# An output projection in three rounded passes one block earlier, with the weight splits that it needs moved into the first block

## The chip, the core and the metric

The kernel runs on one core of a Trainium2 chip. The metric is the device time of one execution in microseconds (us). Engine names are those of the profile: PE is TensorE (matmuls), PEld its weight loads, DVE is VectorE, ACT is ScalarE, POOL is GpSimd, and SP is SyncE, which here only issues DMAs.

## The reference, cut to what matters

The input `x` is (4, 1024, 512) in fp32. A layernorm `xn` of it goes through a time-mix part with a scan over time, and through a feed-forward part with a GELU, and both are added to `x`.

```python
def _L0_attn_ref(x, time_mix_k, time_mix_r, Wk, Wr, Wv, time_decay, ...):
    xx = concatenate([x[:, 1:2, :], x[:, :-1, :]], axis=1) - x
    k = einsum('btc,hc->bth', x + xx * time_mix_k, Wk)     # HIDDEN = 704
    r = einsum('btc,hc->bth', x + xx * time_mix_r, Wr)
    w = exp(-exp(time_decay))
    # scan over time: state = state * w + relu(k_t); out_t = state * r_t
    out = einsum('bth,ch->btc', out, Wv)
    ...  # layernorm of out with ln_gamma, ln_beta

def _L0_ffn_ref(x, W0, bias0, W1, bias1):                  # N = 2048
    X = x.reshape(-1, H).astype(float16)
    D = dot(X.astype(float32), W0.T) + bias0
    D = gelu(D, approximate=False).astype(float16)
    E = dot(D.astype(float32), W1.T) + bias1
    return E.astype(float16)

xn = layernorm(x)
return x + _L0_attn_ref(xn, ...) + _L0_ffn_ref(xn, ...)
```

All weights are fp32. The hidden width 704 is five tiles of 128 and a half tile of 64.

## The kernel before

**Blocks and chunks.** The 4096 tokens are worked off in eight blocks of 512 (`blocks`, numbered 0 to 7; `LAST` is 7). Inside a block the loop `for n in range(NN)` runs over the 16 chunks of 128 of the feed-forward width. In each chunk PE is given, in this order: `up` for the chunk two ahead (`AHEAD = 2`; 8 matmuls at L817), `down` for chunk n (8 matmuls at L839), and one "piece" of the time-mix part of the same block: a k or r projection, a half tile, or one quarter of the output projection (`out_piece`, at n = 12, 13, 14, 15). The chunk in which this stands is called its stage.

**Exact products from rounded operands.** The fast matmuls here take fp32r operands. A weight is therefore split once into terms: W0 and W1 into a high and a low one (`split`, L190 on ACT, L191 on DVE), Wk, Wr and Wv into three (`split_kr`, `split_wv`: three operations on DVE, two on ACT). Each fp32r matmul is one instruction of one pass; a plain fp32 matmul is one instruction of several passes.

**What block 0 does beside.** Block 0 uses the raw Wk and Wr, and prepares the terms for the others. It loads raw W1 chunks two to three chunks ahead (`load_w1_raw`, L229), splits each (`load_w1`), and stores the terms to device memory (`w1d`). It splits W0; the high term stays on the chip for good (`w0h`). It splits tiles of Wk and Wr (`split_kr`, L256, L264, L266 to L268) and stores their terms (`krd`). From block 1 on, `load_w1` and `load_kr` read them back.

**W0's low term.** It stays on the chip in blocks 0 and 1. `store_w0l(g)` queues the store of one quarter of it (four DMAs of 256 KB, to `w0d`) in block 1 at n = 0, 4, 8 and 12. From block 2 on, `load_w0l` reads it one chunk (256 KB) at a time.

**Output projection.** `RAW_OUT` is 2: blocks 0 and 1 use the raw Wv in plain fp32 (`out_full`, L713: five matmuls for each of the four quarters s; `out_halves`, L725: 64x64 pieces for the half tile). Blocks 2 to 7 use `out_three_pass`: per quarter ten fp32r matmuls into `oa` (L754), five into `ob` (L762) and two more into `ob` (L764). For that, `gated` also splits each state tile g into three terms (`split_x`), and Wv is split in block 1 at n = 11, 12, 13, 13, 13 and 15.

**Order.** The order on every engine is written by hand inside `tc.manual_schedule`. `put(n, fn, ...)` appends work to chunk n; `woven` interleaves it on DVE and ACT with what must follow the previous piece. Stores are not issued where they arise: `split_kr`, `load_w1` and `store_w0l` append them to the list `stores`, and `store_weights()` at the end of the chunk issues the whole list on SP, in order. In a chunk of block 0 the raw load stands ahead of that on the same queue:

```python
            if i == 0 and ahead + 1 < NN:
                load_w1_raw(ahead + 1)
            woven(works, jobs + bg[n])
            if i == 0:
                waiting.append((d, load_w1(*nxt)))
            store_weights()
```

So the work that is put to chunk n (a `split_kr`, say) stands on DVE and ACT ahead of the split of the W1 chunk n + 2.

**Start and end.** `first_inputs` keeps PE turning with `busy` matmuls on zeros until the first transposes of x come. At the end, `finish(LAST, s, ...)` adds quarters s = 0 and 1 on POOL and stores each as two halves; quarters 2 and 3 are done in column halves (`end_by_columns`), each stored alone. All these stores are issued by SP.

Of the kernel before, what the change touches and what calls it, by code (L numbers as in the profile page):

```python
# [17 lines left out]
P = 128  # L18
# [4 lines left out]
def time_mix_and_gelu_ffn(  # L23
# [26 lines left out]

    nc = tc.nc
    B, T, C = x.shape
    HID = wkT.shape[1]
# [4 lines left out]
    NN = N // P  # L61
    Q = 32
    QS = 62
    RAW_OUT = 2
    S = 4096.0
    MASK = -4096

# [16 lines left out]
    def part(name, dtype=F32R, tag="q", bufs=QS):  # L84
        return wide.tile([P, TB], dtype, tag=tag, name=name, bufs=bufs)
# [124 lines left out]
            stores.append((w0l_dram[g][:, :, c, :].bitcast(F32), terms.bitcast(F32)))  # L210

    def load_w0l(i, n):
        if i > 1:
            w0ls[i, n] = part(f"w0l_{i}_{n}", tag="w0l", bufs=3)
            g, k = divmod(n, G)
            src = w0l_dram[g][:, k].rearrange("p c k -> p (c k)")
            nc.sync.dma_start(w0ls[i, n].bitcast(F32), src.bitcast(F32))
# [38 lines left out]
        nc.vector.tensor_scalar(u.bitcast(I32), raw.bitcast(I32), MASK, None, ALU.bitwise_and)  # L256
        return u

    def split_kr(block, kind, h):
        raw = raw_w.pop((kind, h)).rearrange("p c k -> p (c k)")  # L260
        name = f"{kind}_{h}"
        u = truncated(raw, f"wu_{name}")
        d = temp(f"wd_{name}")
        nc.vector.tensor_sub(d, raw, u)  # L264
        terms = [part(f"wt_{name}_{p}", tag="kr", bufs=6) for p in range(3)]
        nc.scalar.copy(terms[0], u)  # L266
        nc.scalar.activation(terms[1], d, AF.Copy, scale=S)
        nc.vector.scalar_tensor_tensor(terms[2], d, -S, u, ALU.mult, ALU.add)  # L268
        for p in range(3):
            stores.append((kr_dram[kind, h][p].bitcast(F32), terms[p].bitcast(F32)))  # L270
        return [t.rearrange("p (c k) -> p c k", c=NC) for t in terms]
# [138 lines left out]
    def first_inputs(xs, behind):  # L410
# [69 lines left out]
        with tc.manual_schedule(  # L480
            engines={nc.scalar.engine, nc.vector.engine, nc.tensor.engine}
        ):
            nc.scalar.activation(dev[:, 1:2], eps_sb, AF.Sqrt)
            busy(9)
            nc.tensor.transpose(mix_t, mix_rows, ident[: 2 * NC, : 2 * NC])
            first_stats()
            nc.scalar.copy(mix_sb, mix_t)
            nc.scalar.activation(rest_sb, mix_t, AF.Identity, bias=1.0, scale=-1.0)
            turned(0)
            busy(1)  # L490
            pks = [bank(f"pk_0_{h}") for h in range(FIRST)]
            groups = [(0,), (1,), (2, 3), ()]
            for tiles, following in zip(groups, groups[1:]):
                cols = slice(tiles[0] * P, (tiles[-1] + 1) * P)
                for c in range(NC):
                    if c == NC // 2 + (tiles == (0,)):
                        for s in following:
                            normalized(s)
                    mixed_first(0, c, cols.start, cols.stop)
                for c in range(NC):  # L500
                    if c == NC - len(following):
                        for s in following:
                            turned(s)
                    products(c, cols)
                if tiles == (0,):
                    stats(2)
                    stats(3)
                elif tiles == (1,):
                    nc.tensor.transpose(late_t, late_rows, ident[: ND + NN, : ND + NN])
            for c in range(NC):  # L510
                scaled, added = mixed_first(1, c, 0, TB)
            nc.scalar.copy(late_sb, late_t)
            nc.scalar.activation(w_sb, w_sb, AF.Exp)
            scaled = nc.scalar.activation(w_sb, w_sb, AF.Exp, scale=-1.0)
# [281 lines left out]
        nc.vector.tensor_add(e16, sum_, (b1_sb if base is None else base)[:, cols])  # L796
        return e16

    def finish(i, s, e16, cols=slice(0, C), stores=1, adder=nc.vector):
        z = zs[i][:, s, :]  # L800
        b, rows = tokens_of(i, s)
        adder.tensor_tensor(z[:, cols], z[:, cols], e16, ALU.add)
        width = (cols.stop - cols.start) // stores
        for c0 in range(cols.start, cols.stop, width):
            cut = slice(c0, c0 + width)
            nc.sync.dma_start(out[b, rows, cut], z[:, cut])


    def up(i, n):
        pd = bank(f"pd_{i}_{n}")  # L810
        g, k = divmod(n, G)
        cols = slice(k * P, (k + 1) * P)
        low = w0ls.pop((i, n)) if i > 1 else None
        for c in range(NC):
            wl = w0l[c, g][:, cols] if i < 2 else low[:, c * P : (c + 1) * P]
            for p, w in enumerate((w0h[c, g][:, cols], wl)):
                nc.tensor.matmul(  # L817
                    pd,
                    w,
                    xf[c],  # L820
                    start=(c == 0 and p == 0),
                    stop=(c == NC - 1 and p == 1),
                )

        def after():
            d16 = const.tile([P, TB], F16, tag="d16", name=f"d16_{i}_{n}")
            nc.scalar.activation(d16, pd, AF.Gelu, bias=b0_sb[:, n : n + 1])  # L827
            if i == LAST and n >= NN - 2:
                d = part(f"d_{i}_{n}")
            else:  # L830
                d = part(f"d_{i}_{n}", tag="d", bufs=3)
            nc.scalar.copy(d, d16)  # L832
            return d

        return after
# [66 lines left out]
    with tc.manual_schedule(engines=engines):  # L902
        for i in range(len(blocks)):
# [6 lines left out]
                bg[n].append(lambda: fn(*args))  # L910

            def fetch_kr(block, kind, h):
                fetch = split_kr if (kind, h) in raw_w else load_kr
                ks[block, kind, h] = fetch(block, kind, h)

            def fetch_x():
                state["x"] = load_x(j, "x")
# [20 lines left out]
            if i == 0:  # L938
# [11 lines left out]
                    put(5 + c, split_w0, 3, c)  # L950
                put(1, stats, *range(NS))
                put(3, lambda: norm_apply(j, state["x"]))
                for n, *which in ((1, 0, 1), (3, 0, 2), (5, 0, 3), (7, 0, 4), (7, 1, 1)):
                    put(n, split_kr, 1, *which)
                put(4, turn, 0, 1)
                put(5, turn, 1, 5)
# [2 lines left out]
                put(9, turn, 11, 16)  # L959
                put(9, load_late_constants)  # L960
                put(12, split_half)
                mix_at = (11, 12, 13, 15)
            else:
                order = [(0, h) for h in range(NF)] + [(1, h) for h in range(NF)]
                for k, (kind, h) in enumerate(order):
                    if k == NF:
                        for half in range(2):
                            piece(half_at[half], half_pass, i, half)
                    piece(full_at[k], three_pass, i, kind, h)
                    if k > 1:  # L970
                        split_here = (kind, h) in raw_w
                        put(full_at[k - 2 + split_here], fetch_kr, i, kind, h)
                xr_at = {1: (2, 3, 4, 5), LAST: (1, 2, 2, 3)}.get(i, (2, 2, 3, 3))
                for c, n in enumerate(xr_at):
                    put(n, split_xr, i, c)
                if j <= LAST:
                    put(1 if i == 1 else 2, fetch_x)
                    for s in range(NS):
                        put(2 + s // 2 if i == 1 else 4, stats, s)
                    put(4 if i == 1 else 5, lambda: norm_apply(j, state["x"]))  # L980
                    turns = (4, 6, 4, 2) if i == 1 else (4, 5, 4, 3)
                    for k in range(sum(turns)):
                        unit = next(n for n in range(4) if k < sum(turns[: n + 1]))
                        put(6 + unit, turn, k, k + 1)
                mix_at = (10, 12, 13, 15) if i == 1 else (10, 12, 13, 14)
            if i == 1:
                for g in range(NN // G):
                    put(4 * g, store_w0l, g)
                for h, n in enumerate((11, 12, 13, 13, 13, 15)):
                    put(n, split_wv, h)  # L990
            for s, n in enumerate(out_at):
                piece(n, out_piece, i, s)
            put(11 if j <= LAST else 2, fetch_residual)
            if j <= LAST:
                for c in range(NC):
                    put((10, 10, 11, 12)[c], x16, j, c)
                for c, n in enumerate(mix_at):
                    early[n].append((j, c))
                    put(n, mixed, j, c)
                    put(n + (n == 10), split_xk, j, c)  # L1000
                put(13, fetch_kr, j, 0, 0)
                put(14, fetch_kr, j, 0, 1)

# [44 lines left out]
    with tc.manual_schedule(engines={nc.tensor.engine, nc.vector.engine}):  # L1048
# [5 lines left out]
        for s in range(NS):  # L1054
            if s in by_columns:
                end_by_columns(s, chunks, bases[s])
                continue
            if s == 0:
                for some in (chunks[:-1], chunks[-1:]):
                    for whole in range(NS):  # L1060
                        if whole not in by_columns:
                            for n, operands in some:
                                down(n, whole, *operands)
            e16 = rounded(LAST, s, pe[s])
            finish(LAST, s, e16, stores=2, adder=nc.gpsimd)


# [41 lines left out]
```

## Time and profile before

| what | value |
|---|---|
| median of 3 runs | 867.98 us (867.32 to 868.24) |
| the profiled execution's own time | 866.75 us |
| span of its core in the profile | 864.9 us |
| granted clock of PE, mean | 0.999 |
| DVE busy | 669.1 us (77%) |
| ACT busy | 430.3 us (50%) |
| POOL busy | 75.2 us (9%) |
| DMA, mean over the span | 227 GB/s |

The profiled execution lasted 866.75 us, of which the profile's span is 864.9; the rest, 1.85 us, lies around the span. All times inside the execution are counted from the span's start. The "busy" of an engine is the sum over its instructions; an engine can be busy nearly always and yet not set the end, or the other way round, which is why the chain of waits is read with it.

### The profile page before, as it was taken

To read this page: it belongs to the slowest core of one execution; us is meant where nothing else is said; L and a number is where in the kernel's file an instruction comes from. 1 tells how busy PE (TensorE), PEld (TensorE's weight loads), DVE (VectorE), ACT (ScalarE), POOL (GpSimd) and SP (SyncE) were. 2 spreads that over 40 slices of the span, in tenths; PEclk is the share of its full clock that TensorE was granted. 3 is DMA by queue.
4 is the path that set the end of the run, shared out by engine and by line. 5 is a ranking of instruction groups with operands and counts; after the bars stand their busy time and mean duration, and the time that the engine had idled before them with its cause. 6 is when DMAs were issued, how large, how long until landed. Compare 5 with 4: busy or idle time off the path is not lost.

```text
span 864.9 us, 11076 instructions
## 1 busy us (share of the span) xinstructions
PE 859.0 (99%) x3734; PEld 684.6 (79%) x3734; DVE 669.1 (77%) x1092; ACT 430.3 (50%) x729; POOL 75.2 (9%) x145
## 2 busy tenths in 40 slices
PE   9999999999999999999999999999999999999997
PEld 8666658887588888888888888888888888888886
DVE  7678866897877978778887888778886887876546
ACT  6855723556544464444635456254553446544422
POOL 1000000000011002000021001100011200200002
PEclk9999999999999999999999999999999999999999
DMA  9777947866577745967559665696656966578524
GB/s 283 279 266 256 326 135 256 292 193 221 182 250 265 234 165 181 309 227 253 176 167 332 212 212 197 206 327 200 218 198 202 319 211 214 170 250 282 189 103 135
DMA packets 101173, 196.59 MB, mean 227 GB/s; under 512 B 11103, under 2 KB 25724, under 8 KB 101116
## 3 DMA queue, kind: packets, MB, share of 16 engines
q1 hardware_dynamic: 100956, 195.74, 67.5%
q8 instruction: 30, 0.49, 0.2%
q14 instruction: 27, 0.22, 0.1%
q10 hardware_dynamic: 160, 0.14, 0.0%
HBM read 167.00 MB, written 28.84 MB: 226 GB/s over the span
## 4 chain that ended last, share of the span: by engine, by line
PE 98%; DVE 1%; DMA 0%; issue 0%; ACT 0%; ACTq 0%
PE pd L817 27%; PE pe L839 26%; PE pa L657 15%; PE pb L408 7%; PE oa L754 6%; PE po L713 4%; PE ob L762 3%; PE ph L686 3%; PE pr L408 2%; PE pk L408 2%; PE ob L764 1%; PE po L725 0%; PE pkr L631 0%; DMA x<-in_L_attn_x 0%; PE end L839 0%; DVE xk L467 0%
## 5 line engine op out<-in xcount | busy, mean ns | idle before, releaser
L839 PE MATMUL pe<-w,d 128*128 128x512 f32 x1008 | 248.8, 389 | 0.0
L839 PEld LDWEIGHTS pe<-w,d 128*128 128x128 f32 x1008 | 189.1, 188 | 39.4
L817 PE MATMUL pd<-xf,w0h 128*128 128x512 f32 x512 | 203.5, 398 | 0.0
L817 PE MATMUL pd<-xf,w0l 128*128 128x512 f32 x512 | 199.3, 389 | 0.0
L827 ACT ACTIVATE d<-pd,late_sb 128x512 f16<-128x512 f32 x128 | 87.8, 686 | 166.9 <-PE pd L817 166.7
L817 PEld LDWEIGHTS pd<-xf,w0h 128*128 128x128 f32 x512 | 96.1, 188 | 25.8 <-issue 4.9
L817 PEld LDWEIGHTS pd<-xf,w0l 128*128 128x128 f32 x512 | 96.2, 188 | 21.7 <-issue 1.9
L670 DVE SCALAR_TENSOR_TENSOR y<-pb,a 128x512 f32<-128x512 f32 x70 | 48.4, 691 | 65.6 <-PE pb L408 64.7
L669 ACT ACTIVATE a<-pa 128x512 f32<-128x512 f32 x70 | 41.9, 598 | 84.1 <-PE pa L657 83.8
L832 ACT CAST d<-d 128x512 fp32r<-128x512 f16 x128 | 79.6, 622 | 4.1
L352 DVE STREAM_TRANSPOSE xnT<-x 32x512 f32<-32x512 f32 x112 | 78.7, 702 | 2.1
L320 POOL TENSOR_SCALAR ry<-mvy 128x1 f32<-128x1 f32 x32 | 17.2, 537 | 432.1 <-DVE mvy L327 432.1
L657 PE MATMUL pa<-hk,kr 128*128 128x512 f32 x140 | 54.5, 389 | 0.0
L657 PE MATMUL pa<-lk,kr 128*128 128x512 f32 x140 | 54.5, 389 | 0.0
L657 PE MATMUL pa<-hr,kr 128*128 128x512 f32 x128 | 49.8, 389 | 0.0
L657 PE MATMUL pa<-lr,kr 128*128 128x512 f32 x128 | 49.8, 389 | 0.0
L754 PE MATMUL oa<-wv,hg 128*128 128x512 f32 x120 | 46.7, 389 | 0.0
L754 PE MATMUL oa<-wv,lg 128*128 128x512 f32 x120 | 46.7, 389 | 0.0
L672 ACT ACTIVATE y<-y 128x512 f32<-128x512 f32 x35 | 22.1, 633 | 47.3 <-DVE y L670 47.3
L408 PE MATMUL pb<-mk,kr 128*128 128x512 f32 x140 | 37.4, 389 | 0.0
L713 PE MATMUL po<-wvraw,g 128*128 128x512 f32 x80 | 35.6, 592 | 0.0
L769 DVE SCALAR_TENSOR_TENSOR oy<-ob,oa 128x512 f32<-128x512 f32 x24 | 16.6, 692 | 23.2 <-PE ob L764 23.2
(167 smaller groups left out, 1332.5 us busy)
## 6 DMA issues: line engine op xcount, KB each, us to landing
w<-w1d SPq DMA_DIRECT2D x110, 512.0 KB, 3.7
kr<-krd SPq DMA_DIRECT2D x201, 256.0 KB, 4.9
w0l<-w0d SPq DMA_DIRECT2D x96, 256.0 KB, 4.3
w1d<-w SPq DMA_DIRECT2D x16, 512.0 KB, 4.0
xres<-in_L_attn_x SPq DMA_DIRECT2D x32, 256.0 KB, 5.0
x<-in_L_attn_x SPq DMA_DIRECT2D x31, 256.0 KB, 5.4
krd<-wt SPq DMA_DIRECT2D x30, 256.0 KB, 2.8
out<-xres SPq DMA_DIRECT2D x28, 256.0 KB, 5.1
```

What stands on the lines that cost most here:

```text
L352: nc.vector.transpose(dst[i * Q : (i + 1) * Q, :, :, j, :], src[j * Q : (j + 1) * Q, :, :, i, :],)
L408: return nc.tensor.matmul(dst, w[:, c, :], src, start=(c == 0), stop=(c == NC - 1))
L657: nc.tensor.matmul(pa, w[p][:, c, :], xs[j, c][p], start=(c == 0 and p == 0), stop=(c == NC - 1 and p == 1),)
L669: nc.scalar.activation(a, pa, AF.Copy, scale=1.0 + 1.0 / S)
L670: nc.vector.scalar_tensor_tensor(y, pb, -1.0 / S, a, ALU.mult, ALU.add)
L686: nc.tensor.matmul(pa, w[:, c].rearrange("p two k -> p (two k)"), xs[j, c][p], start=(c == 0 and p == 0), stop=(c == NC - 1 and p == 1),)
L713: nc.tensor.matmul(pos[s], gs[i, h][:, s * P : (s + 1) * P], wv_raw[h], start=(h == 0), stop=False,)
L754: nc.tensor.matmul(pa, gs[i, h][p][:, cols], wv[h][p], start=(h == 0 and p == 0), stop=(h == NF - 1 and p == 1),)
L817: nc.tensor.matmul(pd, w, xf[c], start=(c == 0 and p == 0), stop=(c == NC - 1 and p == 1),)
L827: nc.scalar.activation(d16, pd, AF.Gelu, bias=b0_sb[:, n : n + 1])
L832: nc.scalar.copy(d, d16)
L839: nc.tensor.matmul(pe[s] if sum_ is None else sum_, d[:, s * P : (s + 1) * P], w1[p][:, cols], start=(n == first and p == 0), stop=(n == e ...
```

## The change

`RAW_OUT` becomes 1, so block 1 takes `out_three_pass` too, and its state tiles are split. Five of the six Wv splits move to block 0 (n = 12, 13, 15, 15, 15), the sixth to block 1 at n = 4. W0's low term is stored in block 0 at n = 1, 2, 13 and 14 and read per chunk from block 1 on. The splits of Wr's tiles 2 and 3 move from block 1 to n = 1 and n = 5 of block 0; that of Wr's tile 4 stays in block 1 and writes to other buffers. In block 1 the splits of xr and the transposes of the next x stand at other chunks. At the start one `busy` matmul stands ahead of the first four transposes and two behind them, where there was one behind. At the end the stores of quarters 0 and 1 are whole and are issued by ACT.

```diff
-    RAW_OUT = 2
+    RAW_OUT = 1
+    WV_FIRST = {0: 12, 1: 13, 2: 15, 3: 15, 5: 15}
...
     def load_w0l(i, n):
-        if i > 1:
+        if i > 0:
...
-    def split_kr(block, kind, h):
+    def split_kr(block, kind, h, **home):
...
-        terms = [part(f"wt_{name}_{p}", tag="kr", bufs=6) for p in range(3)]
+        home = home or dict(tag="kr", bufs=6)
+        terms = [part(f"wt_{name}_{p}", **home) for p in range(3)]
...
+            busy(1)
             turned(0)
-            busy(1)
+            busy(2)
...
-    def finish(i, s, e16, cols=slice(0, C), stores=1, adder=nc.vector):
+    def finish(i, s, e16, cols=slice(0, C), adder=nc.vector, queue=nc.sync):
...
-        width = (cols.stop - cols.start) // stores
-        for c0 in range(cols.start, cols.stop, width):
-            cut = slice(c0, c0 + width)
-            nc.sync.dma_start(out[b, rows, cut], z[:, cut])
+        queue.dma_start(out[b, rows, cols], z[:, cols])
...
-        low = w0ls.pop((i, n)) if i > 1 else None
+        low = w0ls.pop((i, n)) if i > 0 else None
...
-                for n, *which in ((1, 0, 1), (3, 0, 2), (5, 0, 3), (7, 0, 4), (7, 1, 1)):
+                for n, *which in (
+                    (1, 0, 1), (1, 1, 2), (3, 0, 2), (5, 0, 3), (5, 1, 3), (7, 0, 4), (7, 1, 1)
+                ):
                     put(n, split_kr, 1, *which)
...
+                for g, n in enumerate((1, 2, 13, 14)):
+                    put(n, store_w0l, g)
...
-                    if k > 1:
-                        split_here = (kind, h) in raw_w
-                        put(full_at[k - 2 + split_here], fetch_kr, i, kind, h)
-                xr_at = {1: (2, 3, 4, 5), LAST: (1, 2, 2, 3)}.get(i, (2, 2, 3, 3))
+                    if (kind, h) in raw_w:
+                        put(2, fetch_kr, i, kind, h)
+                    elif k > 1:
+                        put(full_at[k - 2], fetch_kr, i, kind, h)
+                xr_at = {1: (1, 2, 3, 3), LAST: (1, 2, 2, 3)}.get(i, (2, 2, 3, 3))
...
-                    turns = (4, 6, 4, 2) if i == 1 else (4, 5, 4, 3)
+                    turns = (2, 4, 4, 4, 2) if i == 1 else (0, 4, 5, 4, 3)
...
-            if i == 1:
-                for g in range(NN // G):
-                    put(4 * g, store_w0l, g)
-                for h, n in enumerate((11, 12, 13, 13, 13, 15)):
-                    put(n, split_wv, h)
...
+                for h, n in {0: WV_FIRST, 1: {NF - 1: 4}}.get(i, {}).items():
+                    put(n, split_wv, h)
...
-            finish(LAST, s, e16, stores=2, adder=nc.gpsimd)
+            finish(LAST, s, e16, adder=nc.gpsimd, queue=nc.scalar)
```

More of the change, by code (lines that the diff above doesn't have):

```diff
@@ L812, in up @@
         cols = slice(k * P, (k + 1) * P)
-        low = w0ls.pop((i, n)) if i > 1 else None
+        low = w0ls.pop((i, n)) if i > 0 else None
         for c in range(NC):
-            wl = w0l[c, g][:, cols] if i < 2 else low[:, c * P : (c + 1) * P]
+            wl = low[:, c * P : (c + 1) * P] if i > 0 else w0l[c, g][:, cols]
             for p, w in enumerate((w0h[c, g][:, cols], wl)):
@@ L912, in fetch_kr @@
             def fetch_kr(block, kind, h):
-                fetch = split_kr if (kind, h) in raw_w else load_kr
-                ks[block, kind, h] = fetch(block, kind, h)
+                if (kind, h) in raw_w:
+                    ks[block, kind, h] = split_kr(block, kind, h, tag="q", bufs=QS)
+                else:
+                    ks[block, kind, h] = load_kr(block, kind, h)
             def fetch_x():
@@ L969, in time_mix_and_gelu_ffn @@
                     piece(full_at[k], three_pass, i, kind, h)
-                    if k > 1:
-                        split_here = (kind, h) in raw_w
-                        put(full_at[k - 2 + split_here], fetch_kr, i, kind, h)
-                xr_at = {1: (2, 3, 4, 5), LAST: (1, 2, 2, 3)}.get(i, (2, 2, 3, 3))
+                    if (kind, h) in raw_w:
+                        put(2, fetch_kr, i, kind, h)
+                    elif k > 1:
+                        put(full_at[k - 2], fetch_kr, i, kind, h)
+                xr_at = {1: (1, 2, 3, 3), LAST: (1, 2, 2, 3)}.get(i, (2, 2, 3, 3))
                 for c, n in enumerate(xr_at):
@@ L980, in time_mix_and_gelu_ffn @@
                     put(4 if i == 1 else 5, lambda: norm_apply(j, state["x"]))
-                    turns = (4, 6, 4, 2) if i == 1 else (4, 5, 4, 3)
+                    turns = (2, 4, 4, 4, 2) if i == 1 else (0, 4, 5, 4, 3)
                     for k in range(sum(turns)):
-                        unit = next(n for n in range(4) if k < sum(turns[: n + 1]))
-                        put(6 + unit, turn, k, k + 1)
-                mix_at = (10, 12, 13, 15) if i == 1 else (10, 12, 13, 14)
-            if i == 1:
-                for g in range(NN // G):
-                    put(4 * g, store_w0l, g)
-                for h, n in enumerate((11, 12, 13, 13, 13, 15)):
-                    put(n, split_wv, h)
+                        unit = next(n for n in range(5) if k < sum(turns[: n + 1]))
+                        put(5 + unit, turn, k, k + 1)
+                mix_at = (10, 12, 13, 14)
             for s, n in enumerate(out_at):
```

## The prediction

> **What bounds the kernel now.** I read the page's busy times and its chain of waits first, then the groups by shape, then a table of stages, then the order of single instructions around each moved step.
>
> ```profile
> PE 859.0 (99%) x3734; PEld 684.6 (79%) x3734; DVE 669.1 (77%) x1092; ACT 430.3 (50%) x729; POOL 75.2 (9%) x145
> ...
> PE 98%; DVE 1%; DMA 0%; issue 0%; ACT 0%; ACTq 0%
> ```
>
> PE is busy 859.0 of 864.9 us and carries 98% of the chain. After the first 15 us no gap stands between two matmuls. So the time is the length of the matmul stream, plus about 5 us at its two ends, plus any wait that an edit puts into the stream. Work on DVE, ACT and SP costs nothing until it makes a matmul late.
>
> **What the projection saves.** The groups by shape, then a table of stages (PE, PEld, DVE, ACT, POOL busy, clock, DMA share, GB/s): block 1's four projection stages, then the first one of block 2.
>
> ```profile
> L713 PE MATMUL po<-wvraw,g 128*128 128x512 f32 x80 | 35.6, 592 | 0.0
> ```
> ```profile
> 203.40:210.91 7.51, 7.51 (x27) 4.73 (x26) 6.81 (x13) 5.83 (x10) 0.00 (x0) 1.00 0.76 265
> 210.91:220.40 9.49, 9.49 (x37) 5.09 (x35) 5.45 (x10) 6.51 (x12) 0.00 (x0) 1.00 0.78 237
> 220.40:228.05 7.65, 7.65 (x31) 4.84 (x27) 7.30 (x14) 3.17 (x5) 1.58 (x4) 1.00 0.44 140
> 228.05:237.53 9.48, 9.48 (x37) 5.08 (x35) 7.88 (x14) 4.34 (x7) 0.00 (x0) 1.00 0.48 174
> 312.01:319.49 7.48, 7.48 (x34) 6.19 (x33) 6.34 (x10) 5.43 (x10) 0.00 (x0) 1.00 0.86 292
> ```
>
> Block 1's four sum to 7.51 + 9.49 + 7.65 + 9.48 = 34.13 us. The four of block 2 take 7.48 each, 29.92. The stage that follows takes 6.48 against 6.35, because the first matmuls after fp32 ones come slower. Saving: 34.13 − 29.92 + 0.13 = **4.34 us**. Counted by the matmuls' starts in the trace it is a little less: the fp32 parts take 4 × 4.29 + 2 × 1.03 = 19.22, 68 matmuls at 0.227 from start to start take 15.42, difference 3.80. I take the stages.
>
> **What feeds it.** The built program's order shows the 68 matmuls in place, so the change does what it says. DVE gains in block 1 five splits of g (0.42 + 0.69 + 0.69 each) and loses five splits of Wv of the same three kinds: no change in a block where it is busy some 88 of 105 us, and it is there that its splits of xr and its transposes change places: nothing, with 17 us of slack to cover them. ACT, at 50%, takes the casts that go with these, and POOL's order stays as it was. Five Wv splits enter the end of block 0. DVE's roundings of that block ended at 124.84, and 4.7 us more leaves them near 128.5 to 129.5, while PE needs those banks at 130.77: nothing. Block 1's added reads of W0's low term (16 × 256 KB) replace 16 stores of that size: nothing, as blocks 2 to 7 run without a gap under the same reads; if that cover fails, each late read costs what it is late.
>
> **First new wait: chunk 3 of block 0.** The new split of a Wr tile at n = 1 (three operations on DVE, two on ACT) stands ahead of the split of W1's chunk 3. The order of single instructions there (start, duration):
>
> ```profile
> 47.41 0.69 DVE L268 SCALAR_TENSOR_TENSOR wt<-wd,wu 128x512 fp32r<-128x512 f32 x1
> 48.59 0.69 DVE L191 TENSOR_TENSOR w<-w1raw,w 128x512 fp32r<-128x512 f32 x1 [0.48 <-ACT w L190]
> ```
> ```profile
> 47.95 0.61 ACT L190 CAST w<-w1raw 128x512 fp32r<-128x512 f32 x1
> ```
> ```profile
> 49.74 1.98 PE L839 MATMUL pe<-w,d 128*128 128x512 f32 x8
> ```
>
> Now DVE runs the new three from 48.01 to about 49.9, ACT its two to about 49.7. The W1 cast then ends at 50.31, and DVE's low term at 51.04. The second matmul of that `down` needs it and stood at 49.97. Cost: 51.08 − 49.97 = **1.1 us**. Queued behind the waiting matmul is all of PE; queued behind DVE's three are the scan of tile 3 and the W1 split of the next chunk, which the delayed PE covers.
>
> **Second new wait: the queue, then chunk 7.** `store_w0l` at n = 1 and 2 puts eight stores of 256 KB on SP, ahead of W1's chunks 5 and 6. In block 1 such four stores look like this, followed by a load that itself took 1.24 us to issue:
>
> ```profile
> 136.78 3.31 SPq L225 DMA_DIRECT2D w0d<-w0l  x4
> 140.19 1.24 SPq L242 DMA_DIRECT2D w<-w1d  x1
> ```
>
> Its four groups hold SP 3.41, 3.50, 3.76 and 3.48 us. Walking the queue: three new krd stores to 50.7; four w0d stores to 54.1; the w1d store; W1's chunk 5 issued at 55.4 (before: 49.68); four more w0d stores 56.0 to 59.3; the w1d store; chunk 6 issued at 60.6 (before: 51.92). Chunk 5 should land by 60, and its split be done by 61.5, about when PE (already 1.1 late) wants it. Chunk 6 lands at L. By continuous service of the queue (0.68 per 256 KB, 0.8 per w0d store, as landings are spaced in block 1) L is 62.9; by the `out` store behind a w0d group, which landed 5.29 after its issue, 65.9. I take **64.0**, nearer the service rate because the median read of this kind lands 4.2 after issue.
>
> ACT waits for chunk 6 before it goes on: cast at 64.0 (59.01 before), a GELU, a d cast, two w0h casts to 66.8. DVE's last low term of W0, which needs them, ends at 67.65. Then DVE has its list, unchanged but for one more kr split:
>
> ```profile
> 63.80 0.42 DVE L256 TENSOR_SCALAR wu<-wk 128x512 int32<-128x512 int32 x1
> ...
> 65.71 2.85 DVE L352 STREAM_TRANSPOSE xnT<-x 32x512 f32<-32x512 f32 x4
> 68.59 0.69 DVE L191 TENSOR_TENSOR w<-w1raw,w 128x512 fp32r<-128x512 f32 x1
> ```
>
> From 67.65: two kr splits at 1.77 (67.65 to 71.2), four transposes (2.85, to 74.05), chunk 7's low term to 74.75. Its `down` ran from 71.14, the second matmul at 71.37; with the 1.1 already lost, 72.48. Cost: about **2.3 us**. Later I find no more than 0.2: chunk 9 had a slack of 0.18 but DVE idles 1.69 us before it. Both together: T = 1.1 + 2.3 = **3.4 us**, that is 1.1 + max(0, 2.3 + L − 64.0), so 1.1 at L = 61.7, 2.3 at 62.9, 5.3 at 65.9.
>
> If one wait grew to the length where the clock falls, more would follow. In this trace the last matmul ends at 860.0; the clock column reads 1.00 in 862.00 to 863.00 and 0.50 in 863.30 to 864.80, so some 3 us of rest are needed. Neither wait above is that long, and the sum holds nothing for it. The Trainium skill ("TensorE: Matmul & The Clock Gate", Part 1: The HAM clock gate) says that an idle window of about 3.4 us halves the clock and that a busy one of that length restores it; an estimate by that page is 1.7 us more for one such fall.
>
> **The ends.** Start: the extra dummy matmuls stand beside first products that wait for ACT and DVE anyway (pk at 6.87); two passes in front of the transposes can shift these by 0 to 0.4 us; I take +0.1. Tail: the last add ends at 861.34, its second half store is issued at 861.48 as SP's eighth and lands at 863.88, 2.40 later; a store of the same size with the queue still empty took 1.80 (859.10 to 860.90). Two whole stores from another engine leave fewer on the way: gain 0 to 0.6, less the greater size; I take −0.2. Against it stands a rule of the Trainium skill ("DMA: Bandwidth & Descriptors", "Issuing engines are not separate DMA queues"): another issuer saves only the time to issue. By that rule the tail would give about 0.1, since SP held the last store back by no more.
>
> **Sum.** −4.34 + 3.4 + 0.1 − 0.2 = −1.04 us. The profiled execution's own time, 866.75, becomes 865.7. The median of the runs is 867.98, 1.23 above the profiled one; I add the same and predict **866.9 us**. With T from 2.3 to 5.3 this is 865.8 to 868.8. What a measurement can tell from no change is 0.2%, 1.74 us: faster is below 866.24, slower above 869.72.
>
> **Rivals.** *The queue is not late* (L at most 61.7): for it speaks that the stores of krd in block 0 land 2.0 to 2.5 after issue, and that block 0 at n = 1 to 3 has few reads to share with; against it the 3.4 us that each group held SP in block 1. Then T = 1.1, net −3.3, **864.6 us**, faster. *The queue is later still, and the kernel slower*: one mechanism, W1's chunk 6 behind eight scattered stores. A w1d read 10 to 15 us behind such a group, issued at 151.91, landed 6.95 later, the slowest seen. With it L = 67.6, T = 7.0, net +2.6, **870.6 us**. It outweighs the saving from T = 4.4 (L = 65.0) and is slower by the bound from T = 6.2 (L = 66.8). *The change does not do what it says*: excluded by the built order.
>
> **How the numbers follow.** Net is below −1.74 for T under 2.7 (L under 63.3). The queue not late has 0.25; L between 61.7 and 63.3 has 0.11; L from 63.3 to 66.8, which holds my forecast, 0.42; above that 0.22. So faster 0.36, same 0.42, slower 0.22. The range reaches from the first rival less a better tail (864.2) to just short of the second (870.3); the forecast's own is 865.8 to 868.8.
>
> **What would show it.** Right: block 1's projection stages 7.5 us each; a gap of about 1 us ahead of the second matmul of block 0's `down` 3, one of about 2 ahead of that of `down` 7; SP's w1raw load number 6 issued near 60.6. Wrong: no gap at chunk 7 (then the first rival); gaps at chunks 5 or 6 (queue later than walked), gaps in block 1 around its reads of w0l, or a clock below 1.00 after a gap.

## The result, and the profile after

The changed kernel takes 869.88 us in the median of 14 runs (868.44 to 871.59). The kernel before, beside it on the same chips, takes 866.89 us in the median of 14 (866.25 to 868.24). The ratio is 1.0031, with a 95% interval of 1.0024 to 1.0039: 2.1 to 3.4 us slower, where 1.0 us faster was forecast (866.9, counted from the first three runs of the kernel before, whose median is 867.98). The profiled execution lasted 869.59 us with a span of 867.8, against 866.75 and 864.9.

The page of the changed kernel, engines' busy times and the chain of waits:

```profile
PE 859.3 (99%) x3750; PEld 691.8 (80%) x3750; DVE 681.3 (79%) x1112; ACT 437.1 (50%) x740; POOL 79.0 (9%) x145
...
PE 91%; DVE 3%; DMA 3%; SPq 1%; issue 1%; ACT 1%; ACTq 0%; DVEq 0%
```

The first line hides what happened, the second shows it: the chain of PE fell from 98% to 91%, and DVE, DMA and SP's queue now stand in it. PE's busy time did not fall although block 1 gives it less to do. Part of that busy time is work at half clock (a granted clock of 0.50), as will be seen.

The table of stages, block 1's four projection stages (columns as in the prediction):

```profile
211.57:219.05 7.48, 7.48 (x35) 6.19 (x33) 6.49 (x11) 5.17 (x10) 0.00 (x0) 1.00 0.89 295
219.05:226.53 7.48, 7.48 (x35) 6.19 (x33) 6.66 (x12) 5.93 (x12) 1.55 (x2) 1.00 0.34 107
226.53:234.01 7.48, 7.48 (x35) 6.19 (x33) 6.67 (x12) 2.96 (x5) 1.55 (x2) 1.00 0.63 204
234.01:241.49 7.48, 7.48 (x35) 6.19 (x33) 6.16 (x10) 1.91 (x3) 1.35 (x2) 1.00 0.61 219
```

Each takes the 7.48 us that was forecast, so the saving is whole. What follows reads how late each `down` is against the same one of before; between two of them the change of that lateness is what the work between them lost or won. The first matmul of chunk 7's `down` and that of chunk 8's, before and after, show how it is read: 73.68 − 71.14 = 2.54 and 85.47 − 78.21 = 7.26.

```profile
71.14 1.98 PE L839 MATMUL pe<-w,d 128*128 128x512 f32 x8
78.21 1.98 PE L839 MATMUL pe<-w,d 128*128 128x512 f32 x8
```
```profile
73.68 0.51 PE L838 MATMUL pe<-w,d 128*128 128x512 f32 x1
85.47 0.85 PE L838 MATMUL pe<-w,d 128*128 128x512 f32 x3
```

In this profile:

| where | lateness of `down`, from to (us) | won or lost | forecast |
|---|---|---|---|
| start, up to the first `down` | 0 to 1.08 | +1.08 | +0.1 |
| block 0, chunk 3 | 1.08 to 2.41 | +1.33 | +1.1 |
| block 0, chunks 4 to 6 | 2.41 to 2.54 | +0.13 | 0 |
| block 0, chunk 7 | 2.54 to 7.26 | +4.72 | +2.3 |
| from there to block 1's chunk 5 | 7.26 to 8.16 | +0.90 | 0 |
| block 1's projection | 8.16 to 3.82 | −4.34 | −4.34 |
| blocks 2 to 7 | 3.82 to 4.07 | +0.25 | 0 |
| from the last matmul to the end | 4.89 before, 3.73 now | −1.15 | −0.2 |

The sum is +2.9 us, which is the difference of the spans (867.8 − 864.9).

The order of single instructions on PE shows the two waits of block 0, at chunks 3 and 7, and the longer of two in block 1 (in brackets the wait, counted from the end of the matmul before it as the profile models it):

```profile
51.47 0.50 PE L838 MATMUL pe<-w,d 128*128 128x512 f32 x1 [0.49 <-ACT w L190]
52.20 0.98 PE L838 MATMUL pe<-w,d 128*128 128x512 f32 x3 [0.22 <-DVE w L191]
...
73.68 0.51 PE L838 MATMUL pe<-w,d 128*128 128x512 f32 x1
76.84 1.64 PE L838 MATMUL pe<-w,d 128*128 128x512 f32 x4 [2.65 <-DVE w L191]
...
169.03 0.50 PE L816 MATMUL pd<-xf,w0l 128*128 128x512 f32 x1 [0.20 <-DMA w0l<-w0d]
```

The second matmul of chunk 7's `down` starts 3.16 us after the first; without a wait the two stand 0.23 apart, so the stream loses some 2.9 us there, somewhat more than the printed 2.65. DVE's low term of W1 is what it waited for. SP's queue ahead of that (start, duration of the issues, count):

```profile
51.81 3.00 SPq L225 DMA_DIRECT2D w0d<-w0l  x4
55.33 0.39 SPq L225 DMA_DIRECT2D w1d<-w  x1
55.78 0.76 SPq L229 DMA_DIRECT2D w1raw<-in_L_ffn_W  x1
56.60 3.55 SPq L225 DMA_DIRECT2D w0d<-w0l  x4
60.25 1.21 SPq L225 DMA_DIRECT2D w1d<-w  x1
61.51 0.92 SPq L229 DMA_DIRECT2D w1raw<-in_L_ffn_W  x1
```

The last line is W1's chunk 6. It landed at 65.80, 4.29 us after its issue, and ACT stood idle for 3.29 us until then:

```profile
65.90 0.62 ACT L190 CAST w<-w1raw 128x512 fp32r<-128x512 f32 x1 [3.29 <-DMA w1raw<-in_L_ffn_W]
```

And the stages table in the microseconds behind chunk 7's wait: the clock column is 0.50, then 1.00 again.

```profile
77.50:80.00 2.50, 2.50 (x7) 1.90 (x6) 2.50 (x5) 0.65 (x2) 0.56 (x1) 0.50 1.04 395
82.00:83.00 1.00, 1.00 (x4) 0.46 (x3) 0.97 (x2) 0.89 (x2) 0.00 (x0) 1.00 1.01 385
```

### The profile page after: what moved, and what is told of

Read it like the earlier page. It is cut to its first block, busy times and chain, and to the rows that moved or that the text cites. A ratio compares the mean times of both kernels' runs of the same rounds, so it can differ in the third digit from the quotient of the medians.

```text
span 867.8 us, 11184 instructions
## 1 busy us (share of the span) xinstructions
PE 859.3 (99%) x3750; PEld 691.8 (80%) x3750; DVE 681.3 (79%) x1112; ACT 437.1 (50%) x740; POOL 79.0 (9%) x145
## 4 chain that ended last, share of the span: by engine, by line
PE 91%; DVE 3%; DMA 3%; SPq 1%; issue 1%; ACT 1%; ACTq 0%; DVEq 0%
PE pd L816 24%; PE pe L838 24%; PE pa L659 14%; PE oa L756 7%; PE pb L409 7%; PE ob L764 4%; PE ph L688 3%; PE po L715 2%; PE pr L409 2%; DMA w0l<-w0d 2%; PE ob L766 1%; PE pk L409 1%; SPq L225 1%; PE idle L426 1%; DMA w1raw<-in_L_ffn_W 0%
## 5 line engine op out<-in xcount | busy, mean ns | idle before, releaser
L756 PE MATMUL oa<-wv,hg 128*128 128x512 f32 x140 | 54.5, 389 | 0.0
L756 PE MATMUL oa<-wv,lg 128*128 128x512 f32 x140 | 54.5, 389 | 0.0
L659 PE MATMUL pa<-hr,kr 128*128 128x512 f32 x136 | 52.9, 389 | 0.0
L659 PE MATMUL pa<-lr,kr 128*128 128x512 f32 x136 | 52.9, 389 | 0.0
L771 DVE SCALAR_TENSOR_TENSOR oy<-ob,oa 128x512 f32<-128x512 f32 x28 | 19.4, 692 | 25.2 <-PE ob L766 25.2
L409 PE MATMUL pb<-mr,kr 128*128 128x512 f32 x136 | 36.3, 389 | 0.0
```

The costliest lines, as they stand in the source:

```text
L409: return nc.tensor.matmul(dst, w[:, c, :], src, start=(c == 0), stop=(c == NC - 1))
L659: nc.tensor.matmul(pa, w[p][:, c, :], xs[j, c][p], start=(c == 0 and p == 0), stop=(c == NC - 1 and p == 1),)
L756: nc.tensor.matmul(pa, gs[i, h][p][:, cols], wv[h][p], start=(h == 0 and p == 0), stop=(h == NF - 1 and p == 1),)
```

## The experiments

The theory after this reading: the saving is what was forecast, and it is eaten by three waits (chunk 3, chunk 7, block 1's read of W0's low term), by a half clock that the longest of them brings, and perhaps by the start. The rivals are told with each run.

**The stores spread over the chunks.** In place of four stores at n = 1 and four at n = 2, one at each of n = 2 to 9:

```diff
-                for g, n in enumerate((1, 2, 13, 14)):
+                for q in range(2 * NC):
+                    put(2 + q, store_w0l, q // NC, (q % NC,))
+                for g, n in ((2, 13), (3, 14)):
                     put(n, store_w0l, g)
```

> The changed kernel, but the eight stores of W0's first two low quarters are issued one per chunk at n = 2 to 9 of block 0 in place of four at n = 1 and four at n = 2. Theory (the queue makes W1's chunk 6 late, and with it DVE's list up to chunk 7): chunk 6 lands near 62 in place of 65.8, the gap of 2.65 us at chunk 7 is gone, and the half clock behind it too; 4.8 us under the changed kernel, about 865.1. Rival (the second Wr split on DVE alone makes chunk 7 late): the gap stays at 2 us or more and the time within 1 us of the changed kernel's.

Measured: 865.72 us (864.49 to 867.54), ratio 0.9989 [0.9980, 0.9998] to the kernel before beside it. W1's chunk 6 was issued at 55.21 (61.51 in the changed kernel), and chunk 7's `down` ran through:

```profile
73.59 1.98 PE L838 MATMUL pe<-w,d 128*128 128x512 f32 x8
```

The lateness stayed at 2.45 us from chunk 4 on to block 1, where it had grown by 4.72 in chunk 7 alone. So the stores' place on SP was a condition of that loss. The time stayed 0.6 us above the 865.1 expected; in the profile block 1 lost 1.9 us, where it had lost 0.9 in the changed kernel's.

**The second Wr split moved.** `split_kr` of Wr's tile 3 at n = 10 in place of 5:

```diff
-                    (1, 0, 1), (1, 1, 2), (3, 0, 2), (5, 0, 3), (5, 1, 3), (7, 0, 4), (7, 1, 1)
+                    (1, 0, 1), (1, 1, 2), (3, 0, 2), (5, 0, 3), (10, 1, 3), (7, 0, 4), (7, 1, 1)
```

> The changed kernel, but the split of Wr's tile 3 stands at n = 10 of block 0 in place of n = 5. Theory: DVE's list ahead of chunk 7 is 1.8 us shorter, the gap of 2.65 falls to about 0.9, and that is too short for the clock to fall: both go, 1.8 us of waiting and 2.0 us of half clock, so about 3.8 us under the changed kernel, 866.1. Rival (the clock falls for another reason than the length of this gap): 1.8 us under, 868.1, with a clock of 0.50 still near 78. Rival (queue alone): the gap stays.

Measured: 867.22 us (865.68 to 869.41), ratio 1.0004 [0.9995, 1.0013]. In the profile the wait is 1.01 us:

```profile
74.22 1.88 PE L838 MATMUL pe<-w,d 128*128 128x512 f32 x7 [1.01 <-DVE w L191]
```

The lateness grew there by 1.33 in place of 4.72, and the clock did not fall. So the wait at chunk 7 needs both halves, the late chunk 6 and the split of 1.8 us that then stands in DVE's list; without either the loss is 1.3 us or none. The gain in time was 1.1 us less than expected. The profiled execution, with 869.41 us the slowest of the eleven, lost 4.20 us in block 1, where PE waited 2.29 us and the clock then fell, and 0.49 at chunk 9; what the median execution lost there is not shown.

**The rest filled with matmuls.** Nine small matmuls on zeros between the two matmuls of chunk 7's `down`:

```diff
+            if state.get("fill") and s == 0 and p == 0:
+                for _ in range(9):
+                    nc.tensor.matmul(pe[s][:, :P], zeros, zeros, start=False, stop=False)
```

> The changed kernel with nine small matmuls on zeros (two passes of 0.107 each, 1.9 us in all) added into the sum between the two matmuls of chunk 7's `down` between which PE waits 2.65 us; they add nothing to the sum. Theory (the clock falls because PE rests, in some executions): the wait of 2.65 stays, as DVE sets its end, the clock reads 1.00 up to chunk 8, the shift there grows by 2.7 to 3.1 and not by 4.7, and the time is 1 to 2 us under the changed kernel's, 868 to 869. Rival (the clock falls for what DMA or DVE do then): it falls again in this profile, and the time is not lower.

Measured: 868.93 us (867.68 to 871.70), ratio 1.0021 [1.0011, 1.0032]. In the profile the matmul that DVE releases starts 3.15 us after the first of its `down`, as without the filling, but PE rests only 0.65 of that, and the clock stays up:

```profile
76.00:78.00 2.00, 2.00 (x9) 1.46 (x10) 2.00 (x3) 1.13 (x2) 0.56 (x1) 1.00 1.06 404
```

The lateness rose from 1.53 to 4.59, by 3.06, where it rose by 4.72 in the changed kernel. So the wait alone costs 3.06, and the half clock was the rest. By time alone this run does not settle it, since its interval overlaps that of the changed kernel.

The clock on record does. Beside each execution's time stands its mean granted clock. One spell of half clock lasts 3.4 us and lowers the mean of such an execution by 0.002; a fall behind the last matmul lowers it by 0.001 at most in the profiles. So 0.998 or less is read here as at least one spell inside the execution. All 14 executions of the changed kernel have 0.998 or less; with the rest filled, 10 of 12 have 0.999 or 1.000. (The kernel before, without such waits, has 0.998 or less in 15 of the 73 executions whose clock is on record.) DVE and DMA did the same work in both, so it is PE's rest that brings the half clock.

**Block 1's x fetched later, and nothing else changed.** The reads of x at n = 2 in place of 1, with what follows them:

```diff
-                    put(1 if i == 1 else 2, fetch_x)
+                    put(2, fetch_x)
-                        put(2 + s // 2 if i == 1 else 4, stats, s)
-                    put(4 if i == 1 else 5, lambda: norm_apply(j, state["x"]))
-                    turns = (2, 4, 4, 4, 2) if i == 1 else (0, 4, 5, 4, 3)
+                        put(4, stats, s)
+                    put(5, lambda: norm_apply(j, state["x"]))
+                    turns = (0, 4, 5, 4, 3)
```

> The changed kernel with block 1's x fetched at n = 2, and nothing else changed. Theory: the waits of block 0 stay (chunk 3 about 0.7 us, chunk 7 about 2.65 with the clock falling behind it), those of block 1 (0.9 to 1.6 us where nothing else differs) go: 868.3 to 869.0. Rival: the waits of block 1 stay, and the time is the changed kernel's.

Measured: 868.50 us (866.91 to 869.71), ratio 1.0013 [1.0005, 1.0022], in the range expected. The waits of PE in block 1 fell from 0.31 to 0.15 us and the lateness won there from 0.90 to 0.44. This profile has a second use. Its wait at chunk 7 was 2.66 us, the same as in the changed kernel, but the clock did not fall, and the lateness grew by 3.05 in place of 4.72:

```profile
77.01 1.88 PE L838 MATMUL pe<-w,d 128*128 128x512 f32 x7 [2.66 <-DVE w L191]
```
```profile
77.50:80.00 2.50, 2.50 (x10) 1.54 (x9) 2.50 (x5) 0.82 (x2) 0.56 (x1) 1.00 1.03 390
```

So the half clock does not follow such a wait in every execution; in the two profiles where it came, the loss was 4.72 and 4.46, that is 1.4 to 1.7 us over 3.05. By the mean clocks it comes in most: 9 of the 11 executions here have 0.998 or less, and this profile, with 0.999, is one of the other two.

**No waits in block 0.** The stores spread, Wr's tile 2 split at n = 10 in place of 1, and the old start:

```diff
-                    (1, 0, 1), (1, 1, 2), (3, 0, 2), (5, 0, 3), (5, 1, 3), (7, 0, 4), (7, 1, 1)
+                    (1, 0, 1), (10, 1, 2), (3, 0, 2), (5, 0, 3), (5, 1, 3), (7, 0, 4), (7, 1, 1)
```

> The changed kernel with the old start, with the eight early stores spread one per chunk over n = 2 to 9, and with the split of Wr's tile 2 at n = 10 of block 0 in place of n = 1. Theory: no gap at chunk 3 and none at chunk 7, so what is left is the saving of 4.34, the tail, and block 1's wait for W0's low term near the fourth chunk (0.9 to 4.2 us in the four profiles so far): 3.3 us under the kernel before, 863.7. Rival (the split at n = 10 only moves the wait, as DVE is full up to the end of block 0): a gap after n = 10, and 865 or more.

Measured: 866.29 us (863.51 to 868.24), ratio 0.9986 [0.9975, 0.9998]. The waits of chunks 3 and 7 are gone; the rival's new wait, at chunk 12, is 0.11 us and makes the stream 0.41 later. The profiled execution, 863.80, is as expected. The median is not, and the clock tells the times apart: the four executions with a mean clock of 0.999 or 1.000 took 863.51 to 864.64 us, the eight with 0.998 or less 865.36 to 868.24. So the half clock comes here too, and what the profile still shows of long waits is block 1's:

```profile
156.90 0.50 PE L815 MATMUL pd<-xf,w0l 128*128 128x512 f32 x1 [1.50 <-DMA w0l<-w0d]
```

and on its SP queue that read stands behind four reads of x (1 MB) and one of W1:

```profile
147.40 2.25 SPq L111 DMA_DIRECT2D x<-in_L_attn_x  x4
149.69 0.43 SPq L242 DMA_DIRECT2D w<-w1d  x1
150.17 0.43 SPq L217 DMA_DIRECT2D w0l<-w0d  x1
```

**Both: no waits in block 0, x later in block 1** (the edits of the two runs above together).

> As the kernel with no waits in block 0, and in block 1 the next x is fetched at n = 2 in place of n = 1, with its statistics, normalisation and transposes where blocks 2 to 6 have them. Theory: W0's low term for chunk 6 stood behind four reads of x (1 MB) on the queue; now it stands ahead of them, the gap in block 1 at the fourth chunk is gone, and the time is 5 us under the kernel before, 861.9. Rival (the three stores of a Wk/Wr split at n = 2 of block 1, or block 1's whole load, make it late): a gap of 1 us or more stays in block 1.

Measured: 863.04 us (861.62 to 864.99), ratio 0.9957 [0.9944, 0.9970]. The same read now stands ahead of x, and there is no gap between matmuls after the start anywhere in the profile; four of the five executions have a mean clock of 1.000:

```profile
146.06 0.42 SPq L217 DMA_DIRECT2D w0l<-w0d  x1
147.28 2.00 SPq L300 DMA_DIRECT2D kr<-krd  x3
149.34 2.63 SPq L111 DMA_DIRECT2D x<-in_L_attn_x  x4
152.33 1.79 SPq L225 DMA_DIRECT2D krd<-wt  x3
```

The three krd stores of block 1's split are still at their place, so the rival falls. The time was 1.1 us over what was expected.

**One wait alone.** The same, with Wr's tile 2 split at n = 1 again:

> The kernel with no waits in block 0 and x later, but with the split of Wr's tile 2 back at n = 1. Theory: only the wait at chunk 3 comes back, 0.65 us ahead of its first matmul and 0.3 to 0.6 ahead of its second, and goes to the end undiminished since PE is the bound: 0.7 to 1.3 us over that kernel's 863.04, 864.0. The prediction's term: 1.1. Rival (a wait that early is made good later): within 0.3 us of it.

Measured: 863.49 us (862.79 to 865.22), ratio 0.9957 [0.9941, 0.9973]. In its profile the lateness grows by 1.29 at chunk 3 (1.61 to 2.90) and nothing takes that back later: at the last chunk this profile is 2.70 us behind that of the kernel with both edits, 1.46 from the start and 1.29 from here. By time the two kernels, measured on different chips, can't be told apart (both have the ratio 0.9957); the profiles say 1.3, and the prediction 1.1.

**The start.** Three runs. The changed kernel with the old start:

```diff
-            busy(1)
             turned(0)
-            busy(2)
+            busy(1)
```

> The changed kernel with the start of the kernel before (no dummy matmul ahead of the first four transposes, one behind). In the profile of the changed kernel every matmul of block 0 stands 1.08 us later than before by the first `down` (36.49 against 35.41). Theory: the dummy ahead of the transposes waits for ACT's copy of the mixing weights (5.24 to 5.42) and then holds the transposes back, and the clock opens later; then the first `down` comes back to 35.4 to 35.6 and the time is about 1.0 us under the changed kernel's (868.9 where that has 869.9). Rival: the start of that one execution was late because x landed later (its statistics on DVE began 0.4 us later); then at most 0.6 us goes.

Measured: 870.95 us (869.07 to 871.78), ratio 1.0044 [1.0031, 1.0056]: not faster, though in its profile the first `down` came only 0.13 us late. Its block 1 lost 1.6 us. The kernel before with the new start:

> The kernel before with the start of the changed one alone (one dummy matmul ahead of the first four transposes, two behind). So far the profiles with the new start have the first `down` 1.08, 1.17 and 0.24 us later than in the profile of the kernel before, those with the old start 0.13 and 0.20; the passes become short at 9.2, 9.4 and 7.3 us against 7.0 to 7.2. Theory (the new start makes it likelier that the clock opens one step late): 0.5 to 1 us over the kernel before. Rival (when the clock opens is chance in either form): within 0.3 us of it.

Measured: 867.39 us, ratio 1.0000 [0.9991, 1.0008]. And the fastest kernel with the new start:

> The kernel with no waits in block 0 and x later, but with the changed kernel's start. That kernel took 863.04 us. In five profiles with the new start the first `down` came 1.08, 1.17, 0.24, 0.39 and 1.09 us late, in four with the old one 0.13 to 0.20. Theory (the dummy ahead of the transposes costs 0.7 us on the mean): 863.7. Rival (chance): 863.0, and the first `down` again near 35.6.

Measured: **861.85 us** (861.34 to 863.06), ratio 0.9939 [0.9926, 0.9953], the fastest of all, with the first `down` 0.04 us late. Over all profiles the new start has 1.08, 1.17, 0.24, 0.39, 1.09, 0.08 and 0.04, the old one 0, 0.13, 0.20, 0.16, 0.15 and 1.61. The clock explains part of it. By the traces' record of it, PE gets its full clock at 3.6 to 6.5 us in eleven of the 13 profiles and at 9.1 and 9.3 in two, both with the new start (1.08 and 1.17 late). The late one with the old start had it at 3.83 and lost it again from 7.25 to 10.66:

```profile
7.30:10.60 3.30, 3.24 (x16) 2.95 (x15) 2.97 (x9) 0.00 (x0) 0.79 (x2) 0.50 0.97 290
```

The third late one with the new start (1.09) had the full clock from 3.79; PE waited there for DVE and for reads of Wk (0.30, 0.29 and 0.25 us). So either form can lose 1 us or nothing, and the fastest kernel has the new one. The dummy does wait for ACT, as read; whether the new start makes the loss likelier is open.

**The tail alone**, on the kernel before:

> The kernel before with the tail of the changed one alone (quarters 0 and 1 stored whole, issued by ACT). From the two profiles: before, the end of the span stands 4.90 us after the last matmul's end, in the changed kernel 3.7. Theory: 1.2 us under the kernel before, since four stores fewer share the last 3 us and SP issues each of its own at once. The prediction's term: 0.2 us under.

Measured: 866.34 us, ratio 0.9995 [0.9986, 1.0004], not to be told from no change by time. By the profile the end stands 4.04 us after the last matmul in place of 4.89, and in every profile with all of the change 3.73 to 3.75. The gain of about 1 us is seen in the profiles only, and no run separates the whole stores from the other issuing engine.

## Why the prediction was wrong

**The miss, term by term.** The sum had −1.04 us, the profile has +2.9, a miss of 3.96: chunk 7 +2.42, the start +0.98, block 1 +0.90, chunk 3 +0.23, chunks 4 to 6 and blocks 2 to 7 together +0.38, and the tail −0.95. The medians say the same, −1.04 against +2.99. The forecast time, 866.9, looks nearer to 869.88 than that only because it was counted from 867.98, the median of three runs; over 14 runs the kernel before has 866.89.

**The saving was right:** 4.34 us forecast, 4.34 measured, four stages of 7.48.

**The wait at chunk 3 was right** in place and cause, and a little small: 1.33 (1.29 where it stood alone) against 1.1. The second matmul, which the sum had looked at, stood at 52.20, 1.15 late when the start's 1.08 is taken off, as forecast; most of the rest is lost behind it, where the next two matmuls follow 0.34 and 0.24 us apart.

**The wait at chunk 7 was right, its price was not, and that was the first failed step.** Chunk 6 was forecast to be issued at 60.6 and to land at 64.0 in a stream without the later start; it was issued at 61.51 and landed at 65.80, which is 60.4 and 64.7 with the 1.08 taken off. For a landing at 64.7 the prediction's own formula gives 3.0 in place of 2.3, and 3.05 is what the wait cost where the clock stayed up. So the walk of DVE's list held, and the landing was taken 0.7 too early. The step that failed is the one that said "some 3 us of rest are needed" for the clock to fall, that neither wait is that long, and that the sum holds nothing for it. It rested on one instance, the end of one trace. The ends of all 13 traces, where PE rests for good, show that no one length decides:

```profile
862.10:863.90 1.80, 0.00 (x0) 0.00 (x0) 0.92 (x3) 0.00 (x0) 0.00 (x0) 1.00 0.79 282
864.00:865.70 1.70, 0.00 (x0) 0.00 (x0) 0.00 (x0) 0.00 (x0) 0.00 (x0) 0.50 0.19 65
```
```profile
864.10:867.80 3.70, 0.00 (x0) 0.00 (x0) 0.93 (x3) 0.00 (x0) 0.00 (x0) 1.00 0.48 173
```

The first two rows are from the kernel with x later alone, whose last matmul ends at 862.06: the clock is down 1.9 us later. The third is from the changed kernel, whose last matmul ends at 864.07: it is still up 3.7 us later. In seven profiles the clock fell 1.9 to 3.3 us behind the last matmul, in the other six it had not fallen after 3.7 to 4.0. A rest of 2.65 could thus bring a fall, and by the mean clocks it did in most executions. The 1.7 us which the prediction names for one fall, and leaves out of its sum, is what the fall cost: 4.72 − 3.05 = 1.67.

**Block 1's reads were costed at nothing, and that was the second failed step.** The cover named was that blocks 2 to 7 run without a gap under the same reads. They do, but block 1 fetches the next x one chunk earlier than they, and so its read for chunk 6 is queued behind 1 MB. The profiles with that order lose 0.9 to 4.2 us there, half clock included. The reason given compared the bytes and not the order in the queue.

**The tail was undersized** (0.2 against 1.15). The range given for it ended at 0.6. The last store is now issued 1.02 us after the last matmul's end (1.48 before), and the span ends 2.7 us after that issue (3.4 before): the first part of this, 0.46, was not in the sum at all. The start's 0.1 was far off in this execution, but its runs do not tell it from nothing.

**The signs and the rivals.** The prediction's signs of being wrong include gaps in block 1 around the reads of w0l and a clock below 1.00 after a gap; both came. The rival on the slow side came near in time (870.6) by luck: chunk 6 did not land 6.95 us after its issue but 4.29, and clock and block 1 made the difference. The rival on the fast side leaned on krd stores of block 0 landing 2.0 to 2.5 us after their issue; the trace before has 2.0 to 3.1 for them.

With the three late places removed, the forecast's other terms stand: saving and tail, 4.34 + 1.15, give 5.5 us; the best kernel is 0.61% or 5.3 us faster.

## What to carry to other kernels

Where one engine runs without a gap, each wait put into its stream goes to the end undiminished; so count, for every queue, what a moved DMA now stands ahead of, and spread stores that nobody waits for, one per stage, rather than issue them in a row ahead of loads. "The later blocks do the same" covers a read only if its place in the queue is the same, not just its bytes. And give a wait of some microseconds on PE a price above its length, because the clock can fall behind it.

## What the runs showed of the hardware

The granted clock fell to 0.50 at rests of PE of 2.65 us (0.5 us after its end), 2.67 (0.4 before its end) and 2.29, and stayed up at the same 2.66 in another profile, and at rests of 1.01, 1.50 and 1.61. At the ends of the profiles it fell 1.9 us after the last matmul in one and was still up 4.0 us after it in another. The four spells of half clock that lie inside an execution lasted 3.41 or 3.42 us each. The Trainium skill ("TensorE: Matmul & The Clock Gate", Part 1: The HAM clock gate) gives an idle window of about 3.4 us and says that the window runs freely. The second agrees with a fall that comes by chance, and the length agrees with that of the spells; but the clock was down after 1.9 us of rest, so a wait need not last the whole window.
